# Attention with experts on one core: the first pair's sums of values placed elsewhere, and values ahead of the transposes of short tiles

## The chip, the cores and the metric

The kernel runs on one core of a Trainium2 chip. A core has five engines that run side by side, each through its own instructions in order: TensorE (PE, with the loads of its weights shown as PEld), VectorE (DVE), ScalarE (ACT), GpSimd (POOL) and SyncE (SP), which here issues DMAs. The time is device microseconds of the whole program. The kernel before took 1075.13 us, the median of three runs (1074.84 to 1076.36).

## The reference

The input x is (2, 2048, 512) in f32: two sequences of 2048 tokens. It is normalised, and from the normalised xn come two branches, multiplied and added back:

```python
xn = layernorm(x)
h  = layernorm(xn)
q, k, v = h @ wq, h @ wk, h @ wv                  # 512 wide, one head
p  = softmax(causal(q @ k.T / sqrt(512)))
s  = (p @ v) @ o_proj + xn                        # attention
g  = silu(sum over the top 2 of 8 experts of gate * (silu(xn @ w1.T + b1) @ w2.T + b2))
out = x + s * g
```

Everything is f32.

## The kernel before, in words

The program has three stages. In the first, to about 247 us, the normalised rows are made, the projections are folded (queries and keys into one matrix, values and output projection into another, so that the attention's result needs no further product), and the tokens are routed. To about 610 us the experts run over 68 tiles of routed tokens and write their rows to DRAM. The rest, 610 to 1067 us, is the attention, and the change is there alone.

**The attention** runs over 32 tiles of 128 queries. A tile is named by its place s in the order of work, 0 to 31: first the tiles of one sequence from the longest to the shortest, 15 to 0, then those of the other in the order 8, 9, 0, 1, 6, 7, 2, 3, 4, 5, 10 to 15. A tile sees all keys up to its own, so s=0 has 2048 keys and s=15 has 128. Keys and values are held in blocks of 512 rows (`NBB` = 4 of them: k_0 to k_3, v_0 to v_3), and each block of 512 columns of a tile's scores takes one bank of PSUM.

One loop over s, written out by hand, sets the order of the work on every engine; nothing is reordered after that. What a step issues, in order:

- *scores* of tile s on TensorE (`chunk_scores`, L994, ps), with a mask of the last 128 columns and a running maximum on VectorE (L999, L982);
- the copies that put the previous tile's transposed exponentials together (`join_p`, L1170; the list `joins`), interleaved with the scores;
- for a short previous tile `turn_p`: see below;
- `end_scores` (nm, L1082), `divisor` (ri, L1318 and L1319);
- `exponentials` (L1138, ScalarE): exp of the scores from PSUM to pT. GpSimd then splits each 512 columns into high and low halves (pu, L1148), SyncE transposes them by DMA (puT), and a join of the next step reads puT;
- `values` of tile s-2 (po, L1188), which needs all of that tile's joins;
- the experts' part, `gate` (L1347, L1348, silu at L1350 on ScalarE) and `gather_y` (indirect DMAs on GpSimd, L1337); `attended` and `emit` (L1355, L1358, L1366, L1367) divide, scale, add x and store, some steps later.

ScalarE has to load a table of functions when it goes from exp to silu and back, which is a row of its own (L1350 or L1138, ACT_TABLE_LOAD).

**Short tiles.** A tile of up to 384 keys (`by_te`: s = 13, 14, 15, 18, 19 and 22) isn't transposed by DMA but on TensorE: `turn_p(s)`, at the next step, transposes its pT through a bank of PSUM (pt, L1165), and ScalarE copies the bank back (L1166). In step s before the change TensorE did the scores of s, then pt of s-1, then po of s-2.

**Pairs.** Of the pairs of tiles (s, s+1), those named in `FAST` = (0, 1, 2, 3, 13, 14, 15) take seven products of half size in place of eight, with sums of operands made before, and of results after. For the scores that is `fast_scores` (L1046, seven products p7; L1052, VectorE's adds), which takes a list of things to issue between the adds. For the values it is:

- `combine_v(b, parts)` (vT, L1210): four differences of blocks of v, for blocks 0 to 2 here; part 1 is v12-v11, part 2 v22-part 1, part 3 v22-v12, part 4 v21-part 2;
- `combine_p(s, blocks, parts)` (L1231): s1 = a21+a22, then a21 in place = a11-a21 (called s3 below), s2 = s1-a11, s4 = a12-s2, where the a's are halves of the pair's pT. With `blocks`, each of parts 2 to 4 is followed by the same part of `combine_v` for each block;
- `values_first`: p12, two chains on TensorE (L1240, and L1188 for what is beyond the blocks), a copy of one half by ScalarE (L1268), and VectorE's add of the halves into o_0 (L1257), after which the bank of p12 is free;
- `values_next`: p57, s1 with part 1 of vT, s3 with part 3;
- `values_end`: p64's lower half (s2 with part 2), adds u2 and u3; p03 in the bank that p12 had (rows of L1188, then s4 with v, then L1188 again); p64's upper half with part 4.

These banks come from a pool of three (`ps_b`; po and p7 use it too), the scores' and pt's from a pool of five (`ps_a`).

The first pair (0, 1) is handled at s=2 and s=3. Before the change step 2 issued, after its exponentials and mx_3: vT part 1 for blocks 0 to 2, s1, s3, vT part 3 three times; step 3, after the maxima and nm_3: s2, vT part 2 three times, s4, vT part 4 three times, ri_2, exponentials, o_0's add, joins of tile 2, and the adds of `values_end`. All are VectorE's.

Of the kernel before, what the change touches and what calls it, by code (L numbers as in the profile page):

```python
# [15 lines left out]
ALU = mybir.AluOpType  # L16
# [10 lines left out]
def gated_attention_moe(  # L27
# [27 lines left out]
    nc = tc.nc  # L55
# [3 lines left out]
    NT = B * S // P  # L59
# [3 lines left out]
    NBB = S // TB  # L63
# [130 lines left out]
    parts = [raw.tile([P, NK, D], F32, name=f"w_{i}", tag=f"w_{i}") for i in range(4)]  # L194
# [912 lines left out]
    for i in range(NS):  # L1107
        experts_step(i)
        if i >= 8 and i % 2 == 0 and early:
            f, b, c = early.pop(0)  # L1110
# [46 lines left out]
    def by_te(s):  # L1157

        return sum(widths[s]) <= 3 * P

    def turn_p(s):
        n = sum(widths[s])
        pt = ps_a.tile([P, TB], F32, name=f"pt_{s}", tag="a")
        for k in range(n // P):
            nc.tensor.transpose(pt[:, ts(k, P)], turned[s][:, ts(k, P)], ident)  # L1165
        nc.scalar.copy(turned[s][:, :n], pt[:, :n])  # L1166
# [8 lines left out]
    def values(s):  # L1175
        po = ps_b.tile([P, D], F32, name=f"po_{s}", tag="b")
        product(po, s, 0, place_keys(s), slice(0, D))
        outs[s] = po
# [19 lines left out]
    MOST = 2 * (NBB - 1)  # L1198
    avts, psums, combos, seven = {}, {}, {}, {}

    def combine_v(b, parts=(1, 2, 3, 4)):

        v = avs[b].rearrange("p (i h) d -> p i h d", h=2)
        if 1 in parts:
            avts[b] = cp.tile([P, 2, 4, D // 2], F32, name=f"vT_{b}", tag="vT", bufs=NBB - 1)
        t1, t2, t3, t4 = (avts[b][:, :, i, :] for i in range(4))
        b11, b12, b21, b22 = (v[:, :, h, c] for h in range(2) for c in (LO, HI))
        for i, dst, x1, x2 in (1, t1, b12, b11), (2, t2, b22, t1), (3, t3, b22, b12), (4, t4, b21, t2):
            if i in parts:
                nc.vector.tensor_tensor(dst, x1, x2, ALU.subtract)  # L1210

    def combine_p(s, blocks=(), parts=(1, 3, 2, 4)):


        m = min(min(place_keys(s), place_keys(s + 1)) // 2, MOST)
        a1, a2 = (
            turned[s + i][:, : 2 * m * P].rearrange("p (k h q) -> p k h q", h=2, q=P)
            for i in range(2)
        )
        a11, a12, a21, a22 = a1[:, :, 0], a1[:, :, 1], a2[:, :, 0], a2[:, :, 1]  # L1220
        if 1 in parts:
            psums[s] = [
                cp.tile([P, MOST, P], F32, name=f"s{i}_{s}", tag=f"s{i}")[:, :m] for i in (1, 2, 4)
            ]
        s1, s2, s4 = psums[s]
        for i, dst, x1, x2, op_ in (
            (1, s1, a21, a22, ALU.add), (3, a21, a11, a21, ALU.subtract),
            (2, s2, s1, a11, ALU.subtract), (4, s4, a12, s2, ALU.subtract),
        ):
            if i in parts:  # L1230
                nc.vector.tensor_tensor(dst, x1, x2, op_)  # L1231
                for b in blocks:
                    if i > 1:
                        combine_v(b, (i,))
        combos[s] = m, a11, a12, a22, s1, s2, a21, s4

    def chain(dst, a, v, stop=True):
# [23 lines left out]
    def values_first(s):  # L1261
        m, a11, a12, *_ = combos[s]
        p12, p1 = bank(s, "p12"), half_d(s, "p1")
        o1 = op.tile([P, D], F32, name=f"o_{s}", tag="o", bufs=4)
        chain(p12[:, LO], a11, raw(s, 0, LO))
        chain(p12[:, HI], a12, raw(s, 1, LO), stop=False)
        product(p12[:, HI], s, 2 * m, place_keys(s), LO, start=False)
        nc.scalar.copy(p1, p12[:, LO])  # L1268
        add(o1[:, LO], p12[:, HI], p1)
        if s in AHEAD:  # L1270
            emit_ahead(s, o1, LO)
        seven[s] = p1, o1

    def values_next(s):
        _, _, _, _, s1, _, s3, _ = combos[s]
        p57 = bank(s, "p57")
        chain(p57[:, LO], s1, vt(s, 0))
        chain(p57[:, HI], s3, vt(s, 2))
        seven[s] += (p57,)
# [133 lines left out]
    for s in range(NT + OUT + 2):  # L1413
        fast = s // 2 - 1 in FAST
        pair = (s, s + 1) if s // 2 in FAST else (s,)
        if s < NT and (s % 2 == 0 or len(pair) == 1):
            for k in pair:
                if s:
                    begin_scores(k)
                room(k)  # L1420
        n = s // 2 + 1
        if s % 2 == 0 and NQ <= n < NT // 2:
            for c in range(2):
                fetch_q(n, c)
        if s == 0:
            fetch_parts(s, NBB * ND)
            block_sums(0)
        late = []
        for k in range(NT):
            if k not in AHEAD:  # L1430
                wait = 4 - k % 2 if k // 2 in FAST else 3
                if s == k + wait:
                    late.append((attended, k))
                if s == k + wait + 1:
                    emit(k)
        if len(pair) == 1 or s % 2:
            for f, *args in late:
                f(*args)
        for k in range(NT):
            if s == (NT - 1 if k in AHEAD else k + 2 - k % 2 if k // 2 in FAST else k + 1):  # L1440
                fetch_inputs(k)
        if s == NT - 1:
            gather_y(NT - 2)
        joins = []
        for k in () if s == 1 else (0, 1) if s == 2 else (s - 1,):
            if 0 <= k < NT - 1 and not by_te(k):
                joins += [(join_p, k)] * len(halves[k])
        chunks = []
        if s < NT and s != 1:
            chunks = [(k, j) for k in ((1,) if s == 0 else (s,)) for j in direct(k)]  # L1450
        if s == 0:

            for k, j in chunks:
                chunk_scores(k, j)
            chunks = []
        if s < NT and s % 2 == 0 and len(pair) == 2:
            pools = [(ps_b, "b")] * (NBB - 1) + [(ps_a, "a")] if s < 3 else [(ps_a, "a")]
            fast_scores(s, pools, late + joins[:1])
            joins = joins[1:]
            if s == 0:  # L1460
                query_sums(2, nc.gpsimd)
        for k, j in chunks:
            chunk_scores(k, j)
            if s != 3 and joins:
                f, *args = joins.pop(0)
                f(*args)
        if s != 3:
            for f, *args in joins:
                f(*args)
        if 0 <= s - 1 < NT and by_te(s - 1):  # L1470
            turn_p(s - 1)
        if s < NT and s != 1:
            end_scores(s)
        if s == 3:
            combine_p(0, range(NBB - 1), (2, 4))
        elif fast and s % 2 == 0 and 2 < s < NT:
            combine_p(s - 2)
        if 0 <= s - 1 < NT:
            divisor(s - 1)
        if s < NT:  # L1480
            if s != 1:
                exponentials(s)
            if s % 2 == 0 and len(pair) == 2:
                maximum(s + 1, turned[s + 1][:, : 2 * TB], 0)
            if s == 0:
                end_scores(1)
                exponentials(1)
            fetch_parts(s, 4)
            if s in combine:
                combine_v(combine[s])  # L1490
            if 21 <= s < 25:

                block_sums(K, (s - 20,))
            if s % 2 and s > 3 and s // 2 + 1 in FAST:
                query_sums(s + 1, nc.vector)
        if s == 2:
            for b in range(NBB - 1):
                combine_v(b, (1,))
            combine_p(0, range(NBB - 1), (1, 3))
        elif s == 3:  # L1500
            values_first(0)
            values_next(0)
            for f, *args in joins:
                f(*args)
            values_end(0, [lambda: query_sums(s + 1, nc.vector)])
        elif fast and s % 2 == 0:
            values_first(s - 2)

            if s != NT - 2:
                values_next(s - 2)  # L1510
        elif fast and s == NT - 1:
            values_next(s - 3)
            gate(s - 1)
            values_end(
                s - 3, [lambda: join_p(s)] * len(halves[s]) + [lambda: combine_p(s - 1)]
            )
            for k in AHEAD:
                make_ahead(k)
        elif fast:
            values_end(s - 3)  # L1520
        elif 0 <= s - 2 < NT:
            values(s - 2)

        for k in range(0, NT - 2, 2):
            if s == (k + 2 if k + 2 in AHEAD else k + 3):
                gate(k)
        for k in range(0, NT - 2, 2):
            if s == k + 1:
                gather_y(k)
    att.close()  # L1530


# [42 lines left out]
```

## Time and profile before

| what | value |
|---|---|
| median of three runs | 1075.13 us (1074.84 to 1076.36) |
| the profiled execution's own time | 1069.32 us |
| its span | 1067.6 us |
| TensorE busy | 1043.1 us, 98% |
| VectorE busy | 646.9 us, 61% |
| ScalarE, GpSimd busy | 312.3 us, 29%; 428.9 us, 40% |
| mean granted clock of TensorE | 0.995 |

Times in a profile are counted from the start of its span. A row of a timeline has the start, the length, the engine, the line, the operation, what it writes and reads, its size and count, and in brackets how long the engine was idle before it and what ended that. A row of the waits has the engine and line that waited, what for, the sum of the waits, their number and the longest. The granted clock is the share of its full speed at which TensorE was let run. The chain of waits is followed back from the last instruction to what released each.

### The profile page before, as it was taken

The page shows a single profiled execution, that of the slowest core. Times are in us where ns is not written, and L with a number is a line of the kernel's source. Part 1 is how long each engine was busy: PE and PEld are TensorE (multiplying, and loading weights), DVE is VectorE, ACT ScalarE, POOL GpSimd, SP SyncE. Part 2 cuts the span into 40 slices and gives each one's busy share as a digit, 9 for nine tenths or more (in the row PEclk, how much of TensorE's full clock was granted, in tenths as well). Part 3 has the DMA queues.
Part 4 walks back from the last instruction along what each step waited for, and adds up shares of the span by engine and source line. Part 5 has one row for each costly group of instructions (what it writes and reads, how often), then busy time and mean ns, then how long its engine had stood idle before and what let it go on. Part 6 is the DMA issues. An engine that isn't in the chain of part 4 may idle for free.

```text
span 1067.6 us, 12180 instructions
## 1 busy us (share of the span) xinstructions
PE 1043.1 (98%) x3554; PEld 618.0 (58%) x3554; DVE 646.9 (61%) x1230; ACT 312.3 (29%) x643; POOL 428.9 (40%) x466
## 2 busy tenths in 40 slices
PE   7999999999999999999999999999999998999998
PEld 3688885444555555555545446577654544446577
DVE  4798875775433333333345458667655558697686
ACT  3222321212332322323355222122334432422330
POOL 2364240003433333334331144154557666754272
PEclk9999999999999999999999999999999999999999
DMA  8699989936999999999895275345668658644361
GB/s 288 188 257 314 297 250 333 341 128 173 227 226 230 220 236 222 236 220 216 207 184 130 73 206 143 101 112 142 189 169 266 202 181 234 160 122 130 94 155 40
DMA packets 300512, 209.33 MB, mean 196 GB/s; under 512 B 234520, under 2 KB 247576, under 8 KB 299424
## 3 DMA queue, kind: packets, MB, share of 16 engines
q1 hardware_dynamic: 281248, 146.12, 55.0%
q0 software_dynamic: 10560, 35.17, 12.9%
q10 hardware_dynamic: 8640, 27.27, 7.2%
q8 instruction: 30, 0.49, 0.2%
q14 instruction: 34, 0.28, 0.1%
HBM read 92.89 MB, written 60.03 MB: 143 GB/s over the span
## 4 chain that ended last, share of the span: by engine, by line
PE 77%; POOL 6%; DVE 6%; issue 5%; DMA 3%; ACT 2%; SPq 0%; ACTq 0%; DVEq 0%; POOLq 0%
PE py L921 15%; PE ph L882 15%; PE ps L994 9%; PE p L1240 8%; PE p L1046 8%; PE p L400 7%; PE po L1188 3%; PE pj L341 3%; PE pj L346 3%; PE p L1188 2%; PE pw L207 2%; POOL yg L1337 1%; POOL o L1366 1%; DVE vT L1210 1%; DMA zuT<-zu 1%
## 5 line engine op out<-in xcount | busy, mean ns | idle before, releaser
L921 PE MATMUL py<-w,ht 128*128 (+3 forms) x408 | 187.1, 594 | 0.0
L882 PE MATMUL ph<-w,xT 128*128 (+1 forms) x544 | 173.1, 460 | 0.7 <-POOL keep L1103 0.7
L929 DVE COPY y<-py 128x512 f32<-128x512 f32 x68 | 46.9, 690 | 176.9 <-PE py L921 176.9
L994 PE MATMUL ps<-k,q 128*128 128x512 f32 (+3 forms) x416 | 143.0, 495 | 0.0
L1148 POOL COPY pu<-pT 128x1024 uint16<-128x1024 uint16 (+2 forms) x74 | 85.1, 1180 | 139.4 <-ACT pT L1138 75.0
L882 PEld LDWEIGHTS ph<-w,xT 128*128 128x128 f32 (+1 forms) x544 | 97.3, 181 | 73.3 <-issue 34.3
L907 ACT ACTIVATE ht<-ht,b1sel 128x128 f32<-128x128 f32 (+3 forms) x237 | 73.1, 375 | 224.1 <-DVE ht L901 224.1
L892 POOL COPY hu<-h 128x704 uint16<-128x704 uint16 x68 | 52.6, 773 | 203.7 <-ACT h L890 121.3
L921 PEld LDWEIGHTS py<-w,ht 128*128 128x128 f32 (+3 forms) x408 | 73.4, 182 | 75.5 <-issue 37.9
L994 PEld LDWEIGHTS ps<-k,q 128*128 128x128 f32 x416 | 75.1, 190 | 69.9 <-issue 59.5
L768 POOL DMA_INDIRECT xs<-zu_d,toki x68 | 69.2, 1017 | 69.3 <-DVE toki L642 57.9
L1188 PE MATMUL po<-v,pT 128*128 128x512 f32 x182 | 84.1, 611 | 0.0
L1337 POOL DMA_INDIRECT yg<-y_d,posi x64 | 63.6, 994 | 40.1 <-DVE yg L1348 26.0
L264 POOL COPY zu<-z 128x1024 uint16<-128x1024 uint16 x32 | 35.2, 1100 | 77.9 <-DVE z L249 77.9
L1170 DVE COPY pT<-puT 128x1024 uint16<-128x1024 uint16 (+2 forms) x74 | 53.9, 761 | 6.8 <-DMA puT<-pu 6.8
L1188 PEld LDWEIGHTS po<-v,pT 128*128 128x128 f32 x182 | 35.1, 197 | 39.3 <-issue 37.6
L413 DVE TENSOR_TENSOR so<-p,so 128x512 f32<-128x512 f32 x70 | 45.8, 686 | 14.5 <-DMA v_d<-so 7.6
L842 DVE COPY xT<-xhT 128x1024 uint16<-128x1024 uint16 x68 | 47.4, 697 | 10.5 <-PE ph L882 5.8
L1358 DVE SCALAR_TENSOR_TENSOR o<-xo,xscale,o 128x512 f32<-128x512 f32 x30 | 28.3, 950 | 42.0 <-ACT o L1355 38.9
L1138 ACT ACTIVATE pT<-ps,nm 128x512 f32<-128x512 f32 (+3 forms) x52 | 30.0, 581 | 65.9 <-DVE nm L1082 46.8
L1052 DVE TENSOR_TENSOR pT<-p,pT 128x512 f32<-128x512 f32 x49 | 32.8, 687 | 25.5 <-PE p L1046 16.2
L1138 ACT ACTIVATE pT<-pT,nm 128x1024 f32<-128x1024 f32 x14 | 16.1, 1149 | 107.6 <-DVE nm L1082 70.4
(245 smaller groups left out, 1698.5 us busy)
## 6 DMA issues: line engine op xcount, KB each, us to landing
y_d<-y SPq DMA_DIRECT2D x68, 256.0 KB, 4.0
zu_d<-zu SPq DMA_DIRECT2D x32, 264.0 KB, 5.7
x<-in_x_dram SPq DMA_DIRECT2D x32, 256.0 KB, 5.2
kt_d<-kT ACTq DMA_DIRECT2D x8, 1024.0 KB, 6.3
k<-kt_d SPq DMA_DIRECT2D x32, 256.0 KB, 4.7
q<-qt_d SPq DMA_DIRECT2D x32, 256.0 KB, 5.3
v<-v_d SPq DMA_DIRECT2D x32, 256.0 KB, 5.2
xo<-in_x_dram SPq DMA_DIRECT2D x32, 256.0 KB, 3.9
```

What stands on the lines that cost most here:

```text
L400: nc.tensor.matmul(ps[:, r, :], lhsT=lhs[:, c, ts(r, P)], rhs=rhs[:, c, :], start=(c == 0), stop=(c == 1),)
L768: nc.gpsimd.indirect_dma_start(out=xs, out_offset=None, in_=zu_d, in_offset=bass.IndirectOffsetOnAxis(ap=toki[:, i : i + 1], axis=0),)
L882: nc.tensor.matmul(ph[at, :], lhsT=xT[:, c, at], rhs=rhs[k], start=(c == 0), stop=(c == ND - 1),)
L907: nc.scalar.activation(ht[:hn, c, at], ht[:hn, c, at], AF.Silu, bias=b1sel[:hn, c, j : j + 1])
L921: nc.tensor.matmul(py[at, :], lhsT=ht[:k, c, at], rhs=rhs[n], start=(c == 0), stop=(c == NH - 1),)
L994: nc.tensor.matmul(ps[:, :w], lhsT=aqs[seq[s] // 2][:, c, ts(t % 2, P)], rhs=aks[first + j][:, c, :w], start=(c == 0), stop=(c == ND - 1),)
L1046: nc.tensor.matmul(ps, lhsT=x[:, c], rhs=y[:, c], start=(c == 0), stop=(c == ND // 2 - 1))
L1148: nc.gpsimd.tensor_copy(pu[:, : 2 * w].rearrange("p (h d) -> p h d", h=2), turned[s][:, k : k + w].bitcast(U16).rearrange("p (d h) -> p h ...
L1170: nc.vector.tensor_copy(turned[s][:, k : k + w].bitcast(U16).rearrange("p (i t h) -> p i t h", t=P, h=2), puT[:, : 2 * w // P, :].rearrang ...
L1188: nc.tensor.matmul(dst, lhsT=turned[s][:, ts(k, P)], rhs=avs[first + k // BT][:, k % BT, cols], start=(start and k == k0), stop=(k == k1 - 1),
L1240: nc.tensor.matmul(dst, lhsT=a[:, k], rhs=v(k), start=(k == 0), stop=(stop and k == n - 1))
L1337: nc.gpsimd.indirect_dma_start(out=y, out_offset=None, in_=y_d, in_offset=bass.IndirectOffsetOnAxis(ap=posi[k][:, n : n + 1], axis=0),)
```

## The change

Four things change in the loop; no product, no sum and no transfer is added or dropped, and ScalarE's and SyncE's instructions keep their order.

1. Part 1 of `combine_v` for blocks 0 to 2 is issued within `fast_scores(2)`, at the head of the list of joins, of which five items in place of one go there: the first after the adds of the fifth product, the second after a maximum, the rest at the end. So two of the eight joins are issued there in place of one.
2. Part 3 for blocks 0 to 2 is issued on GpSimd, at the end of step 1, behind the gathers of `gather_y(0)`.
3. The first pair's other sums all go to step 3, behind its exponentials: s1, s3, s2, part 2 of vT for the three blocks; then `values_first(0)` with the add that frees p12's bank; then s4 and part 4 of vT; then `values_next(0)`. ri_2 goes ahead of them.
4. Where the previous tile is short (steps 14, 15, 16, 19, 20 and 23), `values(s - 2)` comes before `turn_p(s - 1)`, and isn't repeated at the end of the step.

```diff
--- before.py
+++ after.py
@@ -1198,19 +1198,18 @@
     MOST = 2 * (NBB - 1)
     avts, psums, combos, seven = {}, {}, {}, {}
 
-    def combine_v(b, parts=(1, 2, 3, 4)):
+    def combine_v(b, parts=(1, 2, 3, 4), engine=nc.vector):
 
         v = avs[b].rearrange("p (i h) d -> p i h d", h=2)
-        if 1 in parts:
+        if b not in avts:
             avts[b] = cp.tile([P, 2, 4, D // 2], F32, name=f"vT_{b}", tag="vT", bufs=NBB - 1)
         t1, t2, t3, t4 = (avts[b][:, :, i, :] for i in range(4))
         b11, b12, b21, b22 = (v[:, :, h, c] for h in range(2) for c in (LO, HI))
         for i, dst, x1, x2 in (1, t1, b12, b11), (2, t2, b22, t1), (3, t3, b22, b12), (4, t4, b21, t2):
             if i in parts:
-                nc.vector.tensor_tensor(dst, x1, x2, ALU.subtract)
-
-    def combine_p(s, blocks=(), parts=(1, 3, 2, 4)):
-
+                engine.tensor_tensor(dst, x1, x2, ALU.subtract)
+
+    def combine_p(s, parts=(1, 3, 2, 4)):
 
         m = min(min(place_keys(s), place_keys(s + 1)) // 2, MOST)
         a1, a2 = (
@@ -1229,9 +1228,6 @@
         ):
             if i in parts:
                 nc.vector.tensor_tensor(dst, x1, x2, op_)
-                for b in blocks:
-                    if i > 1:
-                        combine_v(b, (i,))
         combos[s] = m, a11, a12, a22, s1, s2, a21, s4
 
     def chain(dst, a, v, stop=True):
@@ -1455,8 +1451,11 @@
             chunks = []
         if s < NT and s % 2 == 0 and len(pair) == 2:
             pools = [(ps_b, "b")] * (NBB - 1) + [(ps_a, "a")] if s < 3 else [(ps_a, "a")]
-            fast_scores(s, pools, late + joins[:1])
-            joins = joins[1:]
+            if s == 2:
+                joins = [(combine_v, b, (1,)) for b in range(NBB - 1)] + joins
+            now = 5 if s == 2 else 1
+            fast_scores(s, pools, late + joins[:now])
+            joins = joins[now:]
             if s == 0:
                 query_sums(2, nc.gpsimd)
         for k, j in chunks:
@@ -1468,12 +1467,12 @@
             for f, *args in joins:
                 f(*args)
         if 0 <= s - 1 < NT and by_te(s - 1):
+
+            values(s - 2)
             turn_p(s - 1)
         if s < NT and s != 1:
             end_scores(s)
-        if s == 3:
-            combine_p(0, range(NBB - 1), (2, 4))
-        elif fast and s % 2 == 0 and 2 < s < NT:
+        if fast and s % 2 == 0 and 2 < s < NT:
             combine_p(s - 2)
         if 0 <= s - 1 < NT:
             divisor(s - 1)
@@ -1494,11 +1493,15 @@
             if s % 2 and s > 3 and s // 2 + 1 in FAST:
                 query_sums(s + 1, nc.vector)
         if s == 2:
+            pass
+        elif s == 3:
+            combine_p(0, (1, 3, 2))
             for b in range(NBB - 1):
-                combine_v(b, (1,))
-            combine_p(0, range(NBB - 1), (1, 3))
-        elif s == 3:
+                combine_v(b, (2,))
             values_first(0)
+            combine_p(0, (4,))
+            for b in range(NBB - 1):
+                combine_v(b, (4,))
             values_next(0)
             for f, *args in joins:
                 f(*args)
@@ -1518,7 +1521,7 @@
                 make_ahead(k)
         elif fast:
             values_end(s - 3)
-        elif 0 <= s - 2 < NT:
+        elif 0 <= s - 2 < NT and not (s - 1 < NT and by_te(s - 1)):
             values(s - 2)
 
         for k in range(0, NT - 2, 2):
@@ -1527,6 +1530,9 @@
         for k in range(0, NT - 2, 2):
             if s == k + 1:
                 gather_y(k)
+        if s == 1:
+            for b in range(NBB - 1):
+                combine_v(b, (3,), nc.gpsimd)
     att.close()
```

## Prediction

> **What bounds the kernel now.** The page comes first. TensorE has work for 98% of the span, so a gain can come only from TensorE's waits, and from matmuls that run slowly after a wait:
>
> ```profile
> PE 1043.1 (98%) x3554; PEld 618.0 (58%) x3554; DVE 646.9 (61%) x1230; ACT 312.3 (29%) x643; POOL 428.9 (40%) x466
> ```
>
> The waits of TensorE, asked for the two stretches that the change touches (640 to 690 us from the span's start, on the weight-load side; 784 to 912 us, on the matmul side), then name what ends them:
>
> ```profile
> PEld p L1188 <- DVE o L1257: 4.4, 1, 4.4
> PEld p L1240 <- DVE vT L1210: 1.3, 2, 0.8
> PE pt L1165 <- ACT pT L1138: 6.8, 3, 3.4
> ```
>
> The first is the bank that o_0's add has to free for p03; the second p64's first chain waiting for vT2; the third the three transposes pt_14, pt_18 and pt_22, which wait for their tile's exponentials with finished work behind them in the queue. 680 to 784 us shows no such wait.
>
> Third, VectorE's and TensorE's timelines of 649 to 681 us (start, us, what, count). VectorE runs without a gap from the joins to o_0's add, and the add that frees the bank comes last, though p12 was complete at 656.60:
>
> ```profile
> 651.17 3.57 DVE L1210 TENSOR_TENSOR vT<-v 128x512 f32<-128x512 f32 x3
> 654.66 1.78 DVE L1231 TENSOR_TENSOR s<-pT 128x768 f32<-128x768 f32 x1
> 656.48 1.25 DVE L1231 TENSOR_TENSOR pT<-pT,pT 128x768 f32<-128x768 f32 x1
> 657.65 1.88 DVE L1210 TENSOR_TENSOR vT<-v 128x512 f32<-128x512 f32 x3
> ...
> 669.09 0.40 DVE L1257 TENSOR_TENSOR o<-p,p 128x256 f32<-128x256 f32 x1
> ```
>
> ```profile
> 656.60 2.75 PE L1240 MATMUL p<-vT,s 128*128 128x256 f32 x12
> 659.19 2.75 PE L1240 MATMUL p<-vT,pT 128*128 128x256 f32 x12
> 662.37 3.17 PE L1240 MATMUL p<-vT,s 128*128 128x256 f32 x12 [0.43 <-DVE vT L1210]
> 669.55 2.92 PE L1188 MATMUL p<-v,pT 128*128 128x256 f32 x6 [4.01 <-DVE o L1257]
> ```
>
> Those last six take 2.92 us, 0.49 each; the same shape takes 0.22 each at 675.03 (8 in 1.73 us to the next start). So the wait also costs speed, and the stage table shows the granted clock at 0.88 in 670 to 681 us.
>
> Fourth, the same for the short tiles, TensorE then ScalarE:
>
> ```profile
> 848.00 7.89 PE L1188 MATMUL po<-v,pT 128*128 128x512 f32 x18
> 859.61 0.33 PE L1165 MATMUL pt<-ident,pT 128*128 128x128 f32 x1 [1.99 <-ACT pT L1138]
> 859.77 10.45 PE L1188 MATMUL po<-v,pT 128*128 128x512 f32 x20
> 901.35 0.90 PE L1165 MATMUL pt<-ident,pT 128*128 128x128 f32 x3 [3.43 <-ACT pT L1138]
> ```
>
> ```profile
> 876.54 0.37 ACT L1166 COPY pT<-pt 128x256 f32<-128x256 f32 x1 [5.46 <-PE pt L1165]
> 876.93 1.28 ACT L1138 ACT_TABLE_LOAD   x1
> 878.23 0.69 ACT L1138 ACTIVATE pT<-ps,nm 128x512 f32<-128x512 f32 x1
> ```
>
> The 20 of po_17 take 0.52 us each, the 18 of po_16 0.44. And exp(20) at 878.23 stands behind the copy of pt_19, which stands behind po_17 on TensorE. From there to pt_22 at 901.35 the chain of waits has VectorE, GpSimd, ScalarE and DMA in it and TensorE only in passing: what brings exp(20) forward brings pt_22 forward.
>
> **What the Trainium skill says.** "SBUF — State Buffer", Who interferes with whom: a VectorE instruction with two SBUF inputs contends with a GpSimd one that reads SBUF, and the shared ports are held for a whole instruction. The trace agrees: vT takes 0.68 us alone and up to 1.53 beside GpSimd copies. "TensorE: Matmul & The Clock Gate", What's actually happening: about an idle window of 3.4 us halves the clock, for about as long. The trace agrees after waits of 4.01 and 3.43 us, and here after 1.99 us too (0.52 against 0.44). "GPSIMD Engine Reference", 4.1 Engine selection: two-input elementwise work is about 2 times slower there. Here an add of 128x512 takes 1.27 us on GpSimd against 0.68 on VectorE. "ScalarE: Activation LUTs", What ACT_TABLE_LOAD costs: 1283 ns; the trace has 1.28.
>
> **The first pair.** Removed from VectorE between mx_3 and the end: vT1 x3 (3.57 us) and vT3 x3 (1.88). The order after nm_2 becomes mx_3, the maxima and nm_3, ri_2, s1, s3, s2, vT2, o_0's add, s4, vT4.
>
> *vT1* goes between the adds of the seven products at about 638 to 643.5 us. VectorE is idle there for 2.44 us (to 643.84) and GpSimd only issues gathers, so 3 x 0.68 = 2.0 us fit and I cost them at nothing; without that cover, 2.0 us. Behind them in the queue stand adds that free banks for TensorE's scores; those have 2 us of TensorE work before them. The v loads land by 628.7 (last issue 621.9, 6.8 us), 9.6 us ahead.
>
> *vT3* goes to GpSimd behind the four gathers, at 644.9: 3 x 1.27 to 1.7 us, ending 648.7 to 650.0, ahead of pu_2 (GpSimd was idle 6.5 us there) and long before its reader, p57's second chain. Price: the six copies (joins) of 646.25 to 649.81 (0.59 each) may be held up. Lower bound nothing: nm_2 at 649.5. Upper bound: five joins at about 1.2, nm_2 at 652.3. I take 651.5, as several of them will meet one; before it was 649.73.
>
> From nm_2 = 651.5, with contended durations from the rows (mx_3 1.2, masks and maxima 1.4, s1 1.75, s3 1.5, s2 1.35, vT2 2.9): nm_3 654.35 (before 660.70), s1 ends 656.45, s3 657.95, s2 659.3, vT2 662.2, o_0 662.6, s4 664.2, vT4 666.5. pu_2 and pu_3 on GpSimd now fall on these, which is why I take contended values.
>
> TensorE: p12 to 656.60 as before. p57 5.3 (s1 ready at 656.45), to 661.9. p64 LO 2.6, to 664.5 (vT2 ready 662.2). p03's bank is free at 662.6, 1.9 us ahead: first six 6 x 0.216 = 1.3, to 665.8; s4's chain 2.6, to 668.4; eight 1.7, to 670.1; p64 HI 2.6 and 1.3, to 674.0. Before, the next scores began at 680.80. **6.8 us**: 0.43 and 4.01 of wait and 2.4 of slow matmuls. More isn't in it, as nothing is left to wait for; if nm_2 is at its late bound s1 stops TensorE 0.65 us; if every later sum is 20% dearer (1.7 us), about 2 in all. So 4.8 to 6.8. Joins of tile 2, SP's transposes of tile 3 and the next query load move about 3 us earlier with VectorE, and next query sums end at about 673 against 677.3 that TensorE needs. VectorE, ScalarE and GpSimd have slack from 680 to 784 us, so the gain passes on.
>
> **The short tiles.** ScalarE's instructions keep their order; TensorE does po_(s-2) ahead of pt_(s-1). At s=14 and 15: the wait of 1.38 us before pt_14 goes under po_13; 1.7 us earlier on TensorE. pt_15's copy stays at 836.1 and so exp(16), which only follows; exp(17) comes 0.55 us earlier.
> At s=19: ps_19 ends 855.8; po_17 waits for its first join, 856.35 (0.6 us, from 855.91 and the chain before it), then 20 x 0.43 = 8.6, to 865.0. pt_18 at 865.0, its copy at 865.2, 5 us later than before, and exp(19) behind it in ScalarE's queue at 865.45 (before 862.78); table and silu follow, attended(17) 868.2 (before 870.30), so the late copy delays nobody on the path. ps_20 to 871.1, po_18 872.0, pt_19 872.3, copy 872.35, table 1.28, exp(20) 874.05: **4.2 us** earlier (po_17 starts 3.4 earlier and saves 1.85 of slow matmuls, but pt_19 now stands behind po_18, 1.0).
> At s=23 the latency chain, 4.2 us earlier, gives po_21's first join at about 895.05; TensorE is idle 2.1 us there instead of 3.43, and po_21 covers exp(22). pt_22 is late by its length, exp(23) still earlier than 907.08 (904.6). The gain after 902 us stays 4.2, since ScalarE's and VectorE's chains to 934 us carry the same shift. Bounds: 2 (po_17 or po_21 again at half speed) to 6.
>
> **Sum.** 6.8 + 4.2 = 11.0. The profiled execution took 1069.32 us (span 1067.6 and 1.7 around it): 1058.3 after. It lies 5.8 us below the median of the runs, 1075.13; the same difference gives **1064.1**. A change within 0.2% (2.15 us) can't be told from none.
>
> **Rivals.**
> *The short tiles give nothing* (0.20): late copies of pt_18 and pt_22 hold exp(19) and exp(23), a new wait for joins of 17 and 21 takes the place of the old. For it: exp(19) does come 2.7 us later. Against: nothing on TensorE needs tile 19 before 884. 1075.13 - 6.8 = 1068.3.
> *The first pair's wait moves* (0.10): GpSimd holds the ports, s1 or vT2 comes late, and some 3 of 6.8 us remain. For it: TensorE's slack on s1 is 0.15 us. Against: TensorE's waits then are short ones. 1075.13 - 3 - 4.2 = 1067.9.
> *No difference* (0.07): both stalls return, at p64 and at the chain behind s=26, where VectorE is busy without a gap from 933.7. About 1074.
> *Slower* (0.11): the shared ports. GpSimd's differences and copies lie on all of VectorE's first-pair work, and o_0's add slips past where it was. It decides where the add comes 1.9 + 11.0 + 2.15 = 15 us later than worked out, at 677.7. The upper bound of the contention (nm_2 0.8 later, sums 1.7 dearer) is far from it, so most of this 0.11 is what I haven't seen. About 1079.
>
> **Numbers.** My own case has 0.52 (1061 to 1067). With the first two rivals, 0.82 lies in 1060.5 to 1070.5, which also takes in the lower ends of both bounds (4.8 and 2: 1068.3) and the upper (6.8 and 6: 1062.3), with some 2 us for the runs. Faster 0.82, same 0.07, slower 0.11.
>
> **What would show it.** No wait of p L1188 for o L1257 and full clock in 662 to 674 us; scores of tile 4 at 674; exp(3) near 654.5; vT3 on GpSimd near 645 to 650; exp(20) at about 867 (874 less 6.8); waits for pt gone, short ones for joins before po_17 and po_21. Wrong, if nm_2 comes after 653, if TensorE waits over 1 us on s or vT, or if exp(20) isn't earlier than the first pair's shift.

## The result, and the profile after

The changed kernel takes 1057.53 us, the median of four runs (1057.24 to 1059.05). The kernel before stands at 1074.99 over its four (1069.95 to 1076.36), and the ratio is 0.9849, 95% interval 0.9816 to 0.9882. Forecast were 1064.1 us and a range of 1060.5 to 1070.5: faster, as said, but by 17.5 us where 11.0 were forecast, and outside the range.

Profiled execution against profiled execution, the change is much nearer to the working: 1057.82 us after 1069.32, spans 1056.1 and 1067.6, so 11.5 us where 11.0 were worked out. Most of this section is about where these 11.5 lie; the experiments then ask where the rest of the difference between the medians comes from.

The page's busy line of the changed kernel has TensorE 4.3 us less busy, mostly matmuls at full speed in place of slow ones; VectorE's three instructions are GpSimd's now:

```profile
PE 1038.8 (98%) x3554; PEld 616.2 (58%) x3554; DVE 644.1 (61%) x1227; ACT 312.6 (30%) x643; POOL 432.4 (41%) x469
```

The waits of TensorE's matmuls in the changed kernel, 600 us to the end (engine and line that waited, what for, sum, times, longest; its lines from L1236 on are numbered 4 lower than those of the same statements before, and L1231 is now L1230):

```profile
PE p L1046 <- ACT yg L1346: 1.7, 1, 1.7
PE p L1046 <- DVE sq L1014: 1.3, 1, 1.3
PE po L1188 <- DVE pT L1170: 1.2, 1, 1.2
PE py L921 <- DVE w2c L869: 0.9, 1, 0.9
PE p L1236 <- DVE u L1253: 0.6, 1, 0.6
PE p L1046 <- ACT pT L1065: 0.4, 1, 0.4
```

The waits of 4.0 us for the bank and of 6.8 us before the transposes are gone. New are 1.2 us before po_21, where 2.1 were worked out, and 3.4 us at tiles 26 and 28, which the prediction didn't have.

**The first pair.** TensorE's timeline of the changed kernel (start, us, what, count) has no bracket from p57 to the scores of tile 4, which start at 674.29, where 674.0 was worked out:

```profile
657.02 2.75 PE L1236 MATMUL p<-vT,s 128*128 128x256 f32 x12
659.61 2.75 PE L1236 MATMUL p<-vT,pT 128*128 128x256 f32 x12
662.20 2.75 PE L1236 MATMUL p<-vT,s 128*128 128x256 f32 x12
664.79 1.46 PE L1188 MATMUL p<-v,pT 128*128 128x256 f32 x6
...
674.29 3.60 PE L1046 MATMUL p<-k,q 128*128 128x512 f32 x8
```

VectorE's timeline of the same stretch, and GpSimd's row of vT, show why. GpSimd's three differences (645.70 to 649.41) fall on the joins, of which five take 5.57 us; in the kernel before, six took 3.56:

```profile
646.25 3.56 DVE L1170 COPY pT<-puT 128x1024 uint16<-128x1024 uint16 x6
```

Not all five are slower. The first alone takes 3.29 us and ends 0.55 us after the last of GpSimd's differences; the other four then take their usual time. VectorE's timeline of the changed kernel, asked for no more than this join:

```profile
646.66 3.29 DVE L1170 COPY pT<-puT 128x1024 uint16<-128x1024 uint16 x1
```

So nm_2 comes at 652.16 (651.5 was taken, 652.3 was the late bound). The sums then run to plan on the whole (s1 takes 1.35 us for 1.75, vT2 3.97 for 2.9), and o_0's add ends at 663.34, 1.45 us before p03 wants the bank:

```profile
646.66 5.57 DVE L1170 COPY pT<-puT 128x1024 uint16<-128x1024 uint16 x5
652.16 0.14 DVE L1082 TENSOR_REDUCE nm<-mx 128x1 f32<-128x3 f32 x1
...
655.17 1.35 DVE L1230 TENSOR_TENSOR s<-pT 128x768 f32<-128x768 f32 x1
...
659.03 3.97 DVE L1210 TENSOR_TENSOR vT<-v,vT 128x512 f32<-128x512 f32 x3
662.93 0.41 DVE L1253 TENSOR_TENSOR o<-p,p 128x256 f32<-128x256 f32 x1
```

```profile
645.70 3.71 POOL L1210 TENSOR_TENSOR vT<-v 128x512 f32<-128x512 f32 x3
```

**The short tiles.** TensorE's timeline again: po_17 starts as its tile's exponentials are put together, the 20 run at full speed (8.82 us, before 10.45), and at po_21 there is a wait of 1.23 us, where TensorE waited 3.43 us for pt_22 before. But at tile 26 TensorE has caught up with the other engines:

```profile
849.67 8.82 PE L1188 MATMUL po<-v,pT 128*128 128x512 f32 x20
858.33 0.27 PE L1165 MATMUL pt<-ident,pT 128*128 128x128 f32 x1
...
887.53 7.11 PE L1188 MATMUL po<-v,pT 128*128 128x512 f32 x16 [1.23 <-DVE pT L1170]
894.47 0.49 PE L1165 MATMUL pt<-ident,pT 128*128 128x128 f32 x3
...
915.19 5.39 PE L1046 MATMUL p<-tk,sq 128*128 128x512 f32 x12 [1.30 <-DVE sq L1014]
922.29 1.98 PE L1046 MATMUL p<-k,sq 128*128 128x512 f32 x4 [1.71 <-ACT yg L1346]
```

ScalarE's timeline of the changed kernel shows exp(20) at 867.47, and what ends the 1.71 us: the copy of tile 26's first product, which frees the bank that the sixth needs, stands behind a table load and a silu that VectorE's gate let start at 919.41:

```profile
865.78 0.37 ACT L1166 COPY pT<-pt 128x256 f32<-128x256 f32 x1 [3.38 <-PE pt L1165]
866.17 1.28 ACT L1138 ACT_TABLE_LOAD   x1
867.47 0.69 ACT L1138 ACTIVATE pT<-ps,nm 128x512 f32<-128x512 f32 x1
...
919.41 1.28 ACT L1346 ACT_TABLE_LOAD   x1 [4.16 <-DVE yg L1344]
920.71 1.06 ACT L1346 ACTIVATE yg<-yg 128x1024 f32<-128x1024 f32 x1
921.67 0.57 ACT L1065 COPY pT<-p 128x512 f32<-128x512 f32 x1
```

**By stretch.** In all that follows, executions are compared by five stretches of TensorE's timeline, each from one start to the next: from the span's start to the experts' first matmul; from p12 to the scores of tile 4 (the first pair); from the first po, of tile 8, to the first product of tile 26 (the short tiles); from there to the first product of tile 28; from there to the last matmul's end. What lies between them is the same to 0.7 us in every execution traced: experts 350.3 to 351.0, then 39.6 to p12, and 104.0 from the scores of tile 4 to the first po.

| execution | to experts | first pair | short tiles | 26 to 28 | 28 to end | span |
|---|---|---|---|---|---|---|
| before, profiled | 259.2 | 30.95 | 141.1 | 27.5 | 110.3 | 1067.6 |
| after, profiled | 259.6 | 24.18 | 132.0 | 31.0 | 110.8 | 1056.1 |
| before again (a1) | 261.9 | 31.03 | 141.1 | 27.5 | 111.2 | 1070.6 |
| before again (c2) | 260.8 | 31.14 | 140.6 | 27.5 | 110.1 | 1068.2 |
| before again (c3) | 259.4 | 31.15 | 141.2 | 27.5 | 113.4 | 1070.7 |
| before again (c4) | 264.3 | 32.10 | 139.1 | 27.5 | 111.6 | 1072.5 |
| after again (a2) | 263.3 | 24.18 | 132.0 | 31.0 | 109.9 | 1058.4 |
| first pair only (a3) | 259.2 | 24.17 | 139.2 | 27.5 | 110.5 | 1058.6 |
| short tiles only (a4) | 258.9 | 31.15 | 132.0 | 31.0 | 111.7 | 1063.3 |
| late bank (b1) | 258.9 | 28.44 | 132.0 | 31.0 | 110.8 | 1059.7 |
| vT3 on VectorE (b2) | 265.1 | 24.30 | 132.0 | 31.0 | 109.9 | 1060.6 |
| fill, eight (b3) | 259.5 | 32.05 | 141.2 | 27.5 | 113.4 | 1072.1 |
| edits at 26 and 28 (b4) | 259.2 | 24.18 | 132.0 | 28.5 | 110.5 | 1052.7 |
| fill, four (c1) | 259.2 | 29.46 | 139.2 | 27.5 | 111.5 | 1064.8 |

From the first two rows: first pair 6.8 us less, short tiles 9.1 less, tiles 26 to 28 3.5 more, 12.3 in sum, and the ends of the execution 0.8 against it.

### The profile page after: what moved, and what is told of

Read it like the earlier page. It is cut to its first block, busy times and chain, and to the rows that moved or that the text cites. A ratio compares the mean times of both kernels' runs of the same rounds, so it can differ in the third digit from the quotient of the medians.

```text
span 1056.1 us, 12196 instructions
## 1 busy us (share of the span) xinstructions
PE 1038.8 (98%) x3554; PEld 616.2 (58%) x3554; DVE 644.1 (61%) x1227; ACT 312.6 (30%) x643; POOL 432.4 (41%) x469
## 4 chain that ended last, share of the span: by engine, by line
PE 77%; POOL 6%; issue 6%; DVE 5%; DMA 3%; ACT 2%; SPq 0%; ACTq 0%; POOLq 0%; DVEq 0%
PE py L921 16%; PE ph L882 15%; PE p L1236 9%; PE ps L994 8%; PE p L400 7%; PE p L1046 6%; PE pj L341 3%; PE pw L207 3%; PE po L1188 3%; PE pj L346 3%; PE p L1188 2%; POOL yg L1333 2%; POOL pu L1148 1%; DMA zuT<-zu 1%; POOL o L1362 1%
## 5 line engine op out<-in xcount | busy, mean ns | idle before, releaser
L1188 PE MATMUL po<-v,pT 128*128 128x512 f32 x182 | 81.2, 593 | 1.2 <-DVE pT L1170 1.2
L1362 POOL TENSOR_TENSOR o<-o,yg 128x512 f32<-128x512 f32 x30 | 41.8, 1393 | 13.5 <-DVE o L1354 12.5
```

Of the source, the lines that this page charges most:

```text
L1188: nc.tensor.matmul(dst, lhsT=turned[s][:, ts(k, P)], rhs=avs[first + k // BT][:, k % BT, cols], start=(start and k == k0), stop=(k == k1 - 1),
```

## The experiments

### Both kernels again: is the gap between the runs and the profile a fixed one?

The kernel before, unchanged.

> The kernel before, unchanged, to see where its runs of about 1075 us differ from its profiled 1069.3. Theory A (the clock): the long executions have a lower mean granted clock than the 0.995 of the profiled one (5.5 us more at half speed needs 11 us more of half clock, about 0.990), in the stretches of its three long waits; single executions then fall on either value on one chip. Theory B (the chip): all executions here lie together, near 1069.5 or near 1075, with one clock, and the gap is one between chips.

Measured: 14 runs, 1068.93 to 1076.33 us, median 1072.03, clocks 0.993 to 0.995; the runs of the kernel before beside it, 25, span 1069.08 to 1077.10, clocks 0.991 to 0.997. So neither as put. Executions of one program on one chip spread over 8 us, which refutes B; the four runs with the lowest clock (0.991) take 1075.7 us and more, but others of 1075 to 1076 have 0.994, so the clock is a part and not the whole.

The changed kernel, unchanged.

> The changed kernel again, against the kernel before on the same chip. Theory A: 1057 to 1059 in every run, clock 1.0, as it has no wait over 2 us left; the gain over the kernel before is 11 to 12 us where that runs at 1069 and 17 where it runs at 1075. Theory B: a fixed difference of about 12 us to the kernel before, on whichever level both stand.

Measured: 1057.02 to 1063.23, median 1059.04 (6 runs); ratio 0.9873, 0.9846 to 0.9901. It spreads too, by 6 us, which theory A denied. On this chip the ratio is worth 13.6 us at 1072.2, and the changed kernel's first four runs lie in the lower part of this spread. The traced execution (1058.4) owes its excess to the 263.3 us before the experts, where the profiled one had 259.6.

### One part at a time

First pair alone: the changed kernel less its fourth part.

```diff
         if 0 <= s - 1 < NT and by_te(s - 1):
-
-            values(s - 2)
             turn_p(s - 1)
...
-        elif 0 <= s - 2 < NT and not (s - 1 < NT and by_te(s - 1)):
+        elif 0 <= s - 2 < NT:
             values(s - 2)
```

> The kernel before with parts 1 to 3 of the change (the first pair's sums) and the old order of the short tiles. By the prediction's sum 6.8 us under the kernel before, about 1062.5 where that is at 1069.3. Theory A: some of the excess stays (waits of 2.0 and 3.4 us before the transposes remain), so its runs still vary by some us and its clock is under 1.0. Rival (the first pair's wait moves): 3 us only, with a wait of TensorE for s or vT of over 1 us.

Measured: median 1061.54 (1060.28 to 1065.49), ratio 0.9907, 0.9881 to 0.9933, or 7 to 13 us. By stretch, the first pair takes 24.17, as in the changed kernel: 6.8 us as worked out, and no wait for s or vT. The median moved by more, 10.7 us, and the interval leaves 6.8 out. Between the traced executions of the kernel before on this chip and of this one, 1.9 us more lie in the short tiles' stretch and 2.7 ahead of the experts, where nothing was edited. Its timeline of the short tiles shows the same wait before pt_18 and no slow matmuls after it:

```profile
852.30 0.33 PE L1165 MATMUL pt<-ident,pT 128*128 128x128 f32 x1 [1.98 <-ACT pT L1138]
852.46 8.75 PE L1188 MATMUL po<-v,pT 128*128 128x512 f32 x20
```

The same 20 took 10.45 us in the kernel before after a wait of 1.99. So a wait of 2 us may cost 1.7 us of clock on top, or nothing. Of the eight executions traced with the old order of the short tiles, four have 10.45 us here and four 8.75.

Short tiles alone: the kernel before with the fourth part.

```diff
         if 0 <= s - 1 < NT and by_te(s - 1):
+            values(s - 2)
             turn_p(s - 1)
...
-        elif 0 <= s - 2 < NT:
+        elif 0 <= s - 2 < NT and not (s - 1 < NT and by_te(s - 1)):
             values(s - 2)
```

> The kernel before with part 4 of the change alone (values ahead of the transposes of short tiles). By the prediction's sum 4.2 us under the kernel before, about 1065.1 where that is at 1069.3. Theory A: the wait of 4.0 us at p03 remains with its slow matmuls, so runs vary and the clock stays under 1.0. Rival (the short tiles give nothing): within 1 us of the kernel before, with a wait for joins before po_17 as long as the one removed.

Measured: median 1066.44 (1063.37 to 1071.41, 12 runs), ratio 0.9945, 0.9924 to 0.9966, or 3.6 to 8.1 us. By stretch 9.1 us less, and 3.5 given back at tiles 26 to 28: 5.6 where 4.2 was forecast, and the rival falls. Beside the three executions of the old order that take only 139.1 or 139.2 us in this stretch, it is 3.6. The new waits at tiles 26 and 28 appear here without the first pair's edit, so they belong to this part alone:

```profile
PE p L1046 <- ACT pT L1065: 2.1, 2, 1.7
PE p L1046 <- DVE sq L1014: 1.3, 1, 1.3
```

The 6.8 us of one part and the 5.6 of the other make up the 12.3 of the whole change.

### The first pair's steps

The bank freed late: `values_first(0)` behind all sums.

```diff
             combine_p(0, (1, 3, 2))
             for b in range(NBB - 1):
                 combine_v(b, (2,))
-            values_first(0)
             combine_p(0, (4,))
             for b in range(NBB - 1):
                 combine_v(b, (4,))
+            values_first(0)
             values_next(0)
```

> The changed kernel with one step undone: o_0's add, which frees p12's bank, comes after s4 and part 4 of vT as before the change, 3.5 us later by their rows (1.45 and 2.08), at about 666.5. TensorE reaches p03 at 664.8, so by the theory it waits about 2.1 us there: 2 us slower than the changed kernel, 4 if the clock drops after the wait. Rival (the bank was never the limit once the sums left VectorE): no difference, under 0.5 us.

Measured: median 1060.58 (1058.33 to 1063.44). The first pair takes 28.44, 4.3 us more than in the changed kernel. TensorE's timeline of this kernel has both parts of it, 2.31 us of wait and slow matmuls behind (3.77 for twelve that take 2.75 at full speed):

```profile
666.57 2.27 PE L1188 MATMUL p<-v,pT 128*128 128x256 f32 x6 [2.31 <-DVE o L1253]
668.64 3.77 PE L1236 MATMUL p<-v,s 128*128 128x256 f32 x12
```

So more than half of the first pair's 6.8 us depends on the place of one add.

Part 3 of vT on VectorE.

```diff
-            combine_p(0, (1, 3, 2))
+            combine_p(0, (1, 3))
+            for b in range(NBB - 1):
+                combine_v(b, (3,))
+            combine_p(0, (2,))
             for b in range(NBB - 1):
                 combine_v(b, (2,))
...
-        if s == 1:
-            for b in range(NBB - 1):
-                combine_v(b, (3,), nc.gpsimd)
```

> The changed kernel with part 3 of vT back on VectorE (after s3), nothing on GpSimd. The joins then run undisturbed (0.6 us each, nm_2 some 2 us earlier), and three instructions of 0.7 to 1.2 us come back. By the theory o_0's add moves by under 1.5 us, within TensorE's slack of 1.45 us at p03: under 0.5 us of difference. Rival (GpSimd's share is what makes room): o_0's add 2 us or more later, a wait at p03, slower by 0.5 to 2 us.

Measured: median 1058.22 (1055.96 to 1062.38), first pair 24.30. VectorE's timeline of this kernel, whose p12 starts 5.3 us later than the changed one's: the joins are back at 0.59 us each, vT3 costs 3.14, and o_0's add comes 13.4 us after p12's start, against 12.8:

```profile
651.99 2.36 DVE L1170 COPY pT<-puT 128x1024 uint16<-128x1024 uint16 x4
...
661.21 3.14 DVE L1210 TENSOR_TENSOR vT<-v 128x512 f32<-128x512 f32 x3
...
668.82 0.41 DVE L1253 TENSOR_TENSOR o<-p,p 128x256 f32<-128x256 f32 x1
```

GpSimd's share of the change is worth 0.1 us in this stretch: most of the 3.14 us that it takes off VectorE it takes back by holding up one join for 3.29 us.

Does the wait slow the matmuls? The kernel before with unread matmuls in its wait at p03.

```diff
+        if s == 0:
+            fill = ps_a.tile([P, TB], F32, name="fill", tag="a")
+            for _ in range(8):
+                nc.tensor.matmul(fill, lhsT=ident, rhs=avs[0][:, 0, :], start=True, stop=True)
         product(p03[:, LO], s + 1, 2 * m, k2, HI)
```

> The kernel before with eight added matmuls (128x512, into a bank that nothing reads) ahead of p03, which fill 3.4 us of its wait of 4.0. The wait for the bank stays as long; what the fill changes is the clock. By the theory p03 and what follows run at full speed and the next scores start 2.3 us earlier than before the change. Rival (slow matmuls are not due to the wait): nothing gained.

Measured: median 1073.35 (1067.42 to 1077.51), ratio 1.0010, 0.9995 to 1.0024. The expectation had the size wrong: the eight count as sixteen in the profile and took 6.9 us, 2.7 past the freeing of the bank. What follows took 9.5 us from p03 to the next scores, where the kernel before needs 11.1:

```profile
665.52 7.03 PE L1296 MATMUL fill<-v,ident 128*128 128x512 f32 x16
672.38 1.46 PE L1188 MATMUL p<-v,pT 128*128 128x256 f32 x6
```

Half the fill:

```diff
-            for _ in range(8):
+            for _ in range(4):
```

> The fill again at half its size, since each added matmul is two passes and the eight took 6.9 us, past the freeing of the bank. Four of them take 3.4 us, within the wait of 4.0. Theory: a wait of 0.6 us is left at p03, all that follows runs at full speed as with the longer fill (9.5 us from p03 to the next scores, against 11.1 of the kernel before): 1.6 us earlier at the next scores than the kernel before, counted from p12. Rival (the stall's slow matmuls have another cause): 11.1 us again.

Measured: median 1070.56 (1064.91 to 1078.73), ratio 0.9983, 0.9960 to 1.0006, which the times alone can't tell from none. TensorE's timeline of this kernel shows what they can't: the wait is 0.57 us, the six of p03 take 1.56 in place of 2.92, and the stretch is 29.46, 1.5 us under the profiled execution of the kernel before:

```profile
664.82 3.60 PE L1296 MATMUL fill<-v,ident 128*128 128x512 f32 x8
668.99 1.56 PE L1188 MATMUL p<-v,pT 128*128 128x256 f32 x6 [0.57 <-DVE o L1257]
...
678.59 3.60 PE L1046 MATMUL p<-k,q 128*128 128x512 f32 x8
```

The idle time is what slows the matmuls: with work in it that nobody reads, the kernel isn't slower but 1.5 us ahead in this stretch.

### The waits that came new

The changed kernel with the copy of the first product of tiles 26 and 28 on VectorE, and tile 26's query sums issued earlier.

```diff
-        if s == 2:
+        if s in (2, 26, 28):
             nc.vector.tensor_copy(c11, p1)
...
+        if s == 25:
+            query_sums(26, nc.vector)
         for k, j in chunks:
             chunk_scores(k, j)
...
-            if s % 2 and s > 3 and s // 2 + 1 in FAST:
+            if s % 2 and s > 3 and s // 2 + 1 in FAST and s != 25:
                 query_sums(s + 1, nc.vector)
```

> The changed kernel with two edits at the waits that its profile shows in place of the old: for tiles 26 and 28 the copy of the first product is VectorE's (it stood behind gate and silu on ScalarE), and the query sums of tile 26 come one step's maxima earlier on VectorE. The waits of 1.7, 1.3 and 0.4 us go: 3 to 3.5 us under the changed kernel. Rival (the next one in the chain takes over): the query of tile 26 isn't loaded in time, or VectorE's adds come late, and under 1 us is gained.

Measured: median 1056.03 (1052.31 to 1058.06), ratio to the kernel before 0.9862, 0.9836 to 0.9888. That is the lowest median of all kernels here, but its interval overlaps those of the changed kernel (0.9846 to 0.9901) and of the one beside it with vT3 on VectorE (0.9852 to 0.9899), so by the times it isn't shown to be faster. By stretch it is: 28.5 from tile 26 to 28 in place of 31.0, 2.5 us. The expectation of 3 to 3.5 was too high, since the waits of this kernel after 900 us still have 0.9 at tiles 26 and 28, the larger part for a bank that exponentials free:

```profile
PE p L1046 <- ACT pT L1138: 0.7, 1, 0.7
PE p L1236 <- DVE u L1253: 0.6, 1, 0.6
PE p L1046 <- DVE pT L1063: 0.2, 1, 0.2
```

### Where long executions are long

Three more executions of the kernel before, unchanged.

> The kernel before, one execution, for where a long one is long. Theory: the time up to the experts' first matmul (258.9 to 265.1 us in the executions so far) accounts for it, and from there on it takes 808 to 809 us of span as in the two profiled so far. Rival: the attention's stalls differ, and the rest takes 812 us or more in a long execution.

> As the look before it: up to the experts' first matmul anything from 259 to 265 us, from there 808 to 809 us by the theory; 812 us or more in a long execution by the rival.

> As the two looks before it: up to the experts' first matmul anything from 259 to 265 us, from there 808 to 809 us by the theory; 812 us or more in a long execution by the rival.

Measured: 1069.95, 1072.42 and 1074.16 us. The part after the experts' first matmul (span less that start) is 807.4, 811.3 and 808.2. The longest, c4, is long ahead of the experts, as the theory has it: the waits and stages of its first 100 us show TensorE waiting 3.2 us for zT, which VectorE copies from normalised rows that a DMA has transposed, with the clock at 0.91 (last column but two) behind it; in the profiled execution of the kernel before that wait was 0.7 and the clock 1.00.

```profile
PE pg L307 <- DVE zT L290: 3.2, 1, 3.2
```

```profile
60.00:100.00 40.00, 36.81 (x167) 29.37 (x166) 31.19 (x74) 9.10 (x15) 16.29 (x22) 0.91 0.99 276
```

c3 isn't: its first part is short, and it loses 3.1 us in the last stretch. TensorE's timeline there has a wait of 2.12 us for an add of VectorE (0.66 in the profiled execution), and twelve matmuls at two thirds of full speed after it:

```profile
1037.01 4.18 PE L1240 MATMUL p<-vT,pT 128*128 128x256 f32 x12 [2.12 <-DVE u L1257]
```

The add stands in VectorE's queue behind the gate of the last gathered rows. That these rows landed late isn't shown: VectorE's wait for them ends at 1030.66, and in the profiled execution its last one ends at 1033.78. What is long is one multiplication of the gate, 4.00 us against 0.48 for the next one like it, beside three copies of GpSimd that end at 1034.37:

```profile
1030.66 4.00 DVE L1347 TENSOR_SCALAR yg<-yg,share 128x512 f32<-128x512 f32 x1 [1.10 <-DMA yg<-y_d,posi]
1035.36 0.48 DVE L1347 TENSOR_SCALAR yg<-yg,share 128x512 f32<-128x512 f32 x1
```

```profile
1031.37 3.00 POOL L1148 COPY pu<-pT 128x1024 uint16<-128x1024 uint16 x3
```

So the theory holds for c4, about for c2 (0.6 us under its bound), and not for c3. Over the five traced executions of the kernel before, the first part varies by 5.1 us, the last by 3.2, the first pair by 1.2 and the short tiles by 2.0, the last two after waits of the same length.

## Why the prediction was wrong, point by point

**The step that failed** is the last of the sum: "It lies 5.8 us below the median of the runs, 1075.13; the same difference gives 1064.1." It took the distance of one profiled execution from three runs for a constant of the kernel, to be carried over at 5.8 us. In the changed kernel this term measured 0.3 us with the other sign: its profiled execution, 1057.82, lies at the median of its own runs, 1057.53. Single executions of one program differ by more than this term. 81 further runs of the kernel before, on three chips, go from 1067.24 to 1077.10 with a median of 1072.02, and 15 of them are as long as the shortest of the first three (1074.84). With the 11.0 us taken from the profiled 1069.32 the forecast would have been 1058.3. On the chip of the first experiments, with 1072.2 and 1059.04, the gain is 13.2 us by medians.

What makes one execution longer than another is shown in part: the start, where TensorE waits for rows that a DMA has transposed; VectorE's gate in the last stretch; and the clock after waits. Why all of the first three runs lay between 1074.8 and 1076.4 stays open, since none of them was traced. If runs were independent draws from the 81, three such in a row would come about once in 160 times (15/81, cubed), so chance alone explains them badly.

**The first pair** was right to a tenth: 6.8 us, the next scores at 674.29 for 674.0, nm_2 and the add within 0.8 us. Its parts were less so. Of the "2.4 of slow matmuls", 1.6 is the clock (11.1 us from p03 to the scores, 9.5 after), and 0.4 are short waits of p64 for the parts of vT2, which its row of 3.17 us hides; the last 0.3 is no slow matmul but how a wait is counted, from the modelled end of the matmul before it. That vT1 costs nothing held. The price of GpSimd's share was sized about right, nm_2 0.7 us later than taken, but its form was not: "five joins at about 1.2" was the late bound, and it was one join that waited for all three differences. That this share is worth nothing was not seen.

**The short tiles** were sized too small, 4.2 for 5.6 beside the profiled execution. exp(20) came 4.4 us earlier, counted from the first po, and the start of tile 21's joins 5.1. TensorE itself gained more, 9.1 by tile 26, as po_21 runs in the time in which pt_22 had been waited for; the sum noted that po_21 "covers exp(22)" and didn't carry this on. At tile 26 it met the other engines, whose table load and silu start 5.1 us earlier than before, and gave 3.5 back. So the forecast's reason, that the chains of the other engines "carry the same shift" and set what remains, held; the shift was 0.9 larger than worked out, and 0.6 us that the copy behind the silu had had in hand (it ended at 933.71, the sixth product of tile 26 started at 934.31) came on top. What the prediction left out is that TensorE would run ahead and wait there. Part of the 5.6 is chance: the profiled execution of the kernel before had the slow po_17. Against the four executions without it the gain is 3.6 in three and 5.0 in one (c2), where po_21 is slow instead.

**The rivals.** That the first pair's wait moves, and that the short tiles give nothing, are refuted by a3 and a4. Contention making the kernel slower had a point of decision 15 us away; the add came 0.7 us after its worked-out end. The rival of no difference put a new stall behind tile 26 and laid it to VectorE, busy without a gap: the place was right, but VectorE is idle for 2.9 us just there, and TensorE waits for the query's sums and for ScalarE's copy.

**The range** held cases of mechanism and 2 us "for the runs", a quarter of the 8 us over which the runs of the kernel before lay on one chip.

## What to carry to other kernels

Set a gain worked out in a trace against that trace's own execution, and compare kernels stretch by stretch; before carrying it to a median, ask how far executions of the same program lie apart, above all where it starts on DMA. A buffer's release should be issued as soon as its last reader can run, ahead of sums that are wanted later. And where TensorE is moved forward by more than the engines behind it, look for the next place at which it meets them: here more than a third of the short tiles' gain ended there.

## What was not expected of the hardware

A wait of about 2 us slows the matmuls after it in some executions and not in others: po_17's 20 took 10.45 us after 1.99 and 8.75 after 1.98. Waits of 4.0 us at p03 cost 1.6 to 2.7 us more in the five traced executions of the kernel before. Unread matmuls in such a wait remove that cost. GpSimd's differences took 1.26 to 1.27 us each beside VectorE's joins, no longer than its adds elsewhere (1.27), while one join went from about 0.7 to 3.29 us and ended only after all three of them; the five executions traced with this placement have 3.3 to 3.5. In c3 a multiplication of 0.48 us took 4.00 beside three copies of GpSimd. It isn't always a whole group: VectorE's differences beside GpSimd's copies in the kernel before took 1.53 us at most.
